# Three of seven aggregation products of a two-layer graph network split once more, and the GpSimd and VectorE work around them reordered

## The chip, the cores and the metric

The kernel runs on one core of a Trainium2 chip. The metric is the device time of one execution, in microseconds. TensorE (PE in the profile) multiplies, VectorE (DVE), ScalarE (ACT) and GpSimd (POOL) do the elementwise work, and the queue of SyncE (SP) issues most of the transfers between DRAM and the on-chip memory, SBUF. Products land in PSUM, which has eight banks of 512 float32 columns.

## The reference

Two layers on `x`, float32 of shape (8, 2048, 256), with a sparse weighted adjacency matrix `adj` of 2048 x 2048. Everything is computed in float32.

```
# layer 0
A_norm = A + I
deg    = A_norm.sum(0) + A_norm.sum(1) - diagonal(A_norm)
A_hat  = A_norm * rsqrt(deg)[:, None] * rsqrt(deg)[None, :]
agg    = einsum('nm,bmd->bnd', A_hat, x)            # aggregation
h      = relu(batchnorm(agg @ W1.T + b1))           # 256 -> 512
out    = batchnorm(h @ W2.T + b2)                   # 512 -> 256
x      = layernorm(x + out)
# layer 1: attention of four heads, scores masked where adj == 0
q, k, v = split(x @ W)
x      = layernorm(x + softmax(q k^T / 8 + mask) v)
```

## The kernel before

The kernel runs in stages: it reads `adj`, turns it and sums its rows and columns (0 to about 58 us); it aggregates and applies the first linear layer (58 to about 997 us); it applies the second linear layer (to about 1225 us); the rest is the attention. The change lies in the second stage.

**The aggregation.** The adjacency matrix, turned, lies in SBUF in quarters `T[k, (i, j)]`, each of 128 partitions x 8 x 512 (half of the summed nodes by 512 of the output nodes). `k` is 0 or 1: two passes, each with its own 2 x 512 output nodes. A batch of `x` is loaded in halves of 1024 nodes by 128 features, a `Form` of 128 x 8 x 128 (4 KB per partition); there are nine places for forms, `x0` to `x8`, handed out from the list `free`. A unit `(k, b, d)` treats two batches, `b` and `b + 1`, for half `d` of the 256 features; there are 2 x 4 x 2 = 16 units, and the two units of a pair (d = 0, 1) fill the same output tiles `ag`. In a unit the four blocks (two batches by two halves of nodes) are multiplied with the four quarters by Winograd's variant of Strassen's algorithm: seven products in place of eight, with sums and differences ("forms") on both sides. The forms of `x` are `S[v, 1]` to `S[v, 4]`, made by `s1` to `s4` on GpSimd; those of the adjacency are `T[k, 2]` to `T[k, 4]`, made once per pass by `t2` to `t4` on VectorE; `T[k, (0, 1)]` has been replaced by its difference to `T[k, (0, 0)]`. A `product` is eight matmuls of 128 x 128 by 512 columns into one PSUM bank (four banks, `psa`, line 363). Their order is p1, p6, p2, p7, p4, p5, p3; as each ends, VectorE adds it into `ag` with the partial sums u1, u2, u3 (ScalarE copies p1).

**Scaling.** The symmetric normalization is applied to the inputs by `scale` (GpSimd, line 333) and to the outputs by multiplying each 128 x 512 block of `ag` with `dbc` (GpSimd, lines 492, 517, 528, 536).

**The linear layer.** After the second unit of a pair, `linear` multiplies the aggregated pair with `W1`, again by seven products (line 412, banks `psh`), one batch at a time: `linear(.., 1)` at the end of the unit, `linear(.., 0)` after the first product of the next unit (the list `later`). GpSimd makes its four forms per batch (`linear_form`, line 402), VectorE adds into the tiles `h0` and `h1`, two transfers of 1 MB store them, and `bn_stats` is taken.

**The order of the work.** The stage stands under a manual schedule: each engine executes in the order in which the program names the operations, and waits at an operation until what it needs is there. So the loads (SP), the scalings and forms (POOL) and the additions (DVE) keep the order of the code. A place of a form or tile can be written again only once its last reader has finished. At the end of every second unit, `mask_of` (line 186) writes a byte mask of a quarter for the attention, through the tile `m8`. In the last unit of the first pass (`turn`) the quarters of the second pass are fetched (`fetch`), their mask, difference and forms are made (lines 186, 510, 371, 375, 379).

## Time and profile before

| what | us |
|---|---|
| median of three runs | 3534.34 (3533.58 to 3535.65) |
| the profiled execution, its own time | 3534.78 |
| its span in the profile | 3532.8 |
| PE busy in the span | 3497.7 |
| DVE, ACT, POOL busy | 2106.0, 1583.5, 2335.7 |
| POOL busy in 300 to 600 us (aggregation) | 148.96 |
| one product of line 363 (16 records) | 6.86 |
| a POOL operation of 128 x 512 / 128 x 1024 / a scaling of 128 x 1024 | 1.27 / 2.35 / 1.90 |
| a DVE addition of 128 x 512 from PSUM | 0.69 |

An fp32 matmul shows as two records with two weight loads (PEld) beside them. Times in the profile are microseconds from the span's start; a line number is that of the kernel before; "idle before" is the time for which an engine waited, with what released it. The duration of a matmul record includes its way through the array, so that records overlap; the pitch from start to start is what counts.

### The profile page before, as it was taken

The page shows a single profiled execution, that of the slowest core. Times are in us where ns is not written, and L with a number is a line of the kernel's source. Part 1 is how long each engine was busy: PE and PEld are TensorE (multiplying, and loading weights), DVE is VectorE, ACT ScalarE, POOL GpSimd, SP SyncE. Part 2 cuts the span into 40 slices and gives each one's busy share as a digit, 9 for nine tenths or more (in the row PEclk, how much of TensorE's full clock was granted, in tenths as well). Part 3 has the DMA queues.
Part 4 walks back from the last instruction along what each step waited for, and adds up shares of the span by engine and source line. Part 5 has one row for each costly group of instructions (what it writes and reads, how often), then busy time and mean ns, then how long its engine had stood idle before and what let it go on. Part 6 is the DMA issues. An engine that isn't in the chain of part 4 may idle for free. (4 is left out here: it accounts for less than half of the span.)

```text
span 3532.8 us, 55461 instructions
## 1 busy us (share of the span) xinstructions
PE 3497.7 (99%) x22483; PEld 1474.0 (42%) x22483; DVE 2106.0 (60%) x3128; ACT 1583.5 (45%) x1952; POOL 2335.7 (66%) x1588
## 2 busy tenths in 40 slices
PE   8999999999999999999999999999999999999998
PEld 5444444444444443434443444443444344444332
DVE  6224343441446656766766776676676677677666
ACT  5000000000034455665665665566566566566555
POOL 4544374535347647787777687778677777777777
PEclk9999999999999999999999999999999999999999
DMA  9122342221257345666576666566566556565555
GB/s 345 54 78 75 98 149 83 72 81 51 89 197 267 146 93 107 132 125 127 115 148 118 119 134 133 116 137 131 114 132 135 117 122 141 115 120 124 116 108 121
DMA packets 197578, 440.17 MB, mean 125 GB/s; under 512 B 14128, under 2 KB 121152, under 8 KB 186944
## 3 DMA queue, kind: packets, MB, share of 16 engines
q0 software_dynamic: 64656, 239.37, 36.0%
q1 hardware_dynamic: 132048, 196.11, 16.2%
q8 instruction: 178, 2.92, 0.3%
q10 hardware_dynamic: 608, 1.06, 0.1%
q14 instruction: 88, 0.72, 0.1%
HBM read 126.62 MB, written 75.51 MB: 57 GB/s over the span
## 5 line engine op out<-in xcount | busy, mean ns | idle before, releaser
L955 DVE SCALAR_TENSOR_TENSOR prob<-mask,st 128x1024 f32<-128x1024 uint8 x1024 | 1241.8, 1217 | 412.1 <-PE st L943 410.0
L961 ACT ACTIVATE prob<-prob 128x1024 f32<-128x1024 f32 x1024 | 1080.5, 1056 | 738.5 <-DVE prob L955 693.2
L973 PE MATMUL out_ps<-prob,v 64*64 64x512 f32 x8192 | 1066.6, 591 | 3.0 <-DVE ot L1001 2.0
L943 PE MATMUL st<-qt,kt 64*64 64x512 f32 x8192 | 1066.0, 591 | 0.1
L996 POOL TENSOR_TENSOR acc<-acc,prob 128x1024 f32<-128x1024 f32 x317 | 827.7, 2611 | 4.9
L363 PE MATMUL pa<-t,x 128*128 128x512 f32 x1792 | 773.2, 593 | 2.8 <-ACT t L239 2.8
L983 POOL DMA_DIRECT2D prob<-prob x447 | 404.4, 930 | 532.2 <-PE out_ps L973 446.0
L943 PEld LDWEIGHTS st<-qt,kt 64*64 64x64 f32 x8192 | 306.5, 133 | 574.9 <-issue 476.7
L973 PEld LDWEIGHTS out_ps<-prob,v 64*64 64x64 f32 x8192 | 305.6, 133 | 544.2 <-issue 489.9
L363 PEld LDWEIGHTS pa<-t,x 128*128 128x128 f32 x1792 | 340.9, 190 | 431.8 <-issue 427.0
L985 POOL TENSOR_TENSOR acc<-acc,prob 128x1024 f32<-128x1024 f32 x126 | 298.3, 2367 | 9.7
L492 POOL TENSOR_TENSOR ag<-ag,dbc 128x512 f32<-128x512 f32 x16 | 20.3, 1266 | 313.0 <-DVE ag L491 285.9
L472 ACT COPY ag<-pa 128x512 f32<-128x512 f32 x16 | 9.4, 588 | 448.4 <-PE pa L363 432.7
L421 ACT COPY h<-ph 128x512 f32<-128x512 f32 x28 | 16.4, 586 | 416.7 <-PE ph L412 416.7
L994 POOL TENSOR_TENSOR acc<-prob 128x1024 f32<-128x1024 f32 x64 | 171.4, 2677 | 1.0 <-DMA prob<-prob 1.0
L1049 DVE SCALAR_TENSOR_TENSOR x<-pm,ri,x 128x64 f32<-128x64 f32 x512 | 109.5, 276 | 86.2 <-PE pm L1041 86.2
L762 ACT ACTIVATE x<-x,ln_nm,ln_rs 128x256 f32<-128x256 f32 x256 | 137.6, 586 | 7.5 <-POOL ln_nm L758 7.5
L877 PE MATMUL pm<-x1t,wq 128*128 128x512 f32 x272 | 132.5, 610 | 2.6 <-ACT x1t L845 2.4
L891 PE MATMUL pm<-wq,x1t 128*128 128x128 f32 x1024 | 125.1, 275 | 0.0
L891 PEld LDWEIGHTS pm<-wq,x1t 128*128 128x128 f32 x1024 | 119.4, 192 | 2.5 <-ACT x1t L845 1.7
L1001 DVE TENSOR_TENSOR ot<-out_ps,ot 128x512 f32<-128x512 f32 x64 | 44.2, 691 | 126.6 <-ACT ot L1000 126.6
L877 PE MATMUL st<-x1t,wq 128*128 128x512 f32 x240 | 119.0, 618 | 0.0
(161 smaller groups left out, 2944.9 us busy)
## 6 DMA issues: line engine op xcount, KB each, us to landing
prob<-prob POOLq DMA_DIRECT2D x447, 512.0 KB, 4.8
x<-in_x_dram SPq DMA_DIRECT2D x92, 512.0 KB, 6.8
h_d<-h SPq DMA_DIRECT2D x28, 1024.0 KB, 4.2
t<-h_d SPq DMA_DIRECT2D x28, 1024.0 KB, 8.2
a<-in_adj_dram SPq DMA_DIRECT2D x16, 1024.0 KB, 5.2
y_d<-ag SPq DMA_DIRECT2D x32, 512.0 KB, 2.6
out_dram<-x SPq DMA_DIRECT2D x31, 512.0 KB, 3.6
yt<-y_d SPq DMA_DIRECT2D x28, 512.0 KB, 3.3
```

The lines of the kernel that those rows point to most:

```text
L363: nc.tensor.matmul(pa, s.t[:, m, :], t[:, m, :], start=(m == 0), stop=(m == HT - 1))
L762: nc.scalar.activation(self.t[:, i, :], self.t[:, i, :], AF.Identity, bias=self.nm[:, i : i + 1], scale=self.rs[:, i : i + 1],)
L877: nc.tensor.matmul(pm, wq[:, d, wcols], xt[:, d, cols], start=(d == 0), stop=(d == ND - 1))
L891: nc.tensor.matmul(pm[:, j * P : (j + 1) * P], xt[:, d, t * P : (t + 1) * P], wq[:, d, wcols], start=(d == 0), stop=(d == ND - 1),)
L943: nc.tensor.matmul(st[r * HD : (r + 1) * HD, h, :], kt[hs, j * P + r * HD : j * P + (r + 1) * HD], qt[hs, cols], start=True, stop=True,)
L955: nc.vector.scalar_tensor_tensor(p, mask[:, j, cols][:, None, :].to_broadcast([P, 2, CH]), MASKED, st, op0=ALU.mult, op1=ALU.add,)
L961: nc.scalar.activation(probs[g], probs[g], AF.Exp)
L973: nc.tensor.matmul(outs[u][hs, r, :], inp.qkv[b, hp][2][rs, j, hs], probs[g][rs, h, :], start=(j == 0), stop=(j == NT - 1),)
L983: nc.gpsimd.dma_start(probs[g - 1], probs[g], accum_op=ALU.add)
L985: nc.gpsimd.tensor_add(accs[u], accs[u], probs[g])
L994: nc.gpsimd.tensor_add(accs[v], probs[g - 7], probs[g - 5])
L996: nc.gpsimd.tensor_add(accs[v], accs[v], probs[g - 5])
```

## The change

Units with d = 0 now compute only p1, p6, p2 and p7. The other three products are left over for the unit with d = 1, which computes each of them for both units at once, as seven "inner" products: the two forms (of d = 0 and d = 1) are stacked to a 2 x 2 matrix of blocks with the two halves of the summed nodes, and the quarter of the adjacency to one with the halves of its columns. An inner product is four matmuls of 256 columns. Class `Inner` makes the inner forms: of the stacked forms on GpSimd into four tiles `narrow0` to `narrow3` of 128 x 512 (`s12`, `s3`, `s4`), of the quarter on VectorE into two tiles `wide0` and `wide1` of 128 x 1024 (`t2`, `t3`, `t4`). The sums are gathered in a form `sums` and then added to one or two output tiles (`targets`). While one set of inner products runs, the forms of the next (`follower`) are made. `narrow` and `wide` are the former `h0` and `h1` in smaller tiles, stored by six transfers.

With it the order changes. In units with d = 0, the forms of the next unit are scaled after p6. In units with d = 1, the scalings of the next forms come after those of the first inner set, s1 and s3 in the middle of the second set (`aside`), beside the scaling of the output by rows (`by_rows`); a last scaling stands after it, and s2 and s4 after `linear`. At the turn, the mask and the difference of the new quarter are cut into six slices, given out among the inner products (`extra`), and t3 and t4 move behind `linear(.., 0)` of the next unit. The masks of the other quarters are made at the end of units with d = 0, into `wide0`; the first of these units in a pass also replaces the right upper block of three quarters by a difference, in place. There is a tenth place for forms, and `m8` is gone.

```diff
-    free = [f"x{i}" for i in range(9)]
+    free = [f"x{i}" for i in range(10)]
...
-            nc.sync.dma_start(h_d[cs[0]], lo)
+            for f in range(2):
+                nc.sync.dma_start(h_d[cs[0]][:, 2 * f : 2 * f + 2, :], los[f])
...
-            nc.sync.dma_start(h_d[cs[1]], hi)
+            for f in range(NH):
+                nc.sync.dma_start(h_d[cs[1]][:, f, :], hi[f])
...
+        M = HT // 2
+        H2 = CH // 2
+        def inner_t(k, tk, j, c):
+            return T[k, tk][:, j * M : (j + 1) * M, c * H2 : (c + 1) * H2]
+        class Inner:
+            def __init__(self, k, vs, key, tk, e, targets):
+                self.k, self.key, self.tk, self.e, self.targets = k, key, tk, e, targets
+                self.forms = [S[(v, *key)] for v in vs]
+            def a(self, i, j):
+                return self.forms[i].t[:, j * M : (j + 1) * M, :]
+            def b(self, j, c):
+                return inner_t(self.k, self.tk, j, c)
+            def place_t(self, e):
+                return wide(e).rearrange("p a b -> p (a b)").rearrange("p (m n) -> p m n", m=M)
+            def t2(self):
+                self.y2 = self.place_t(self.e)
+                nc.vector.tensor_sub(self.y2, self.b(1, 1), self.b(0, 1))
+            def t3(self):
+                self.y3 = self.place_t(1 - self.e)
+                nc.vector.tensor_sub(self.y3, self.y2, self.b(0, 0))
+            def t4(self):
+                nc.vector.tensor_sub(self.y2, self.b(1, 0), self.y2)
+            def place_s(self, n):
+                return narrow(n).rearrange("p (m n) -> p m n", m=M)
+            def s12(self):
+                self.x1, self.x2 = self.place_s(0), self.place_s(1)
+                nc.gpsimd.tensor_add(self.x1, self.a(1, 0), self.a(1, 1))
+                nc.gpsimd.tensor_sub(self.x2, self.x1, self.a(0, 0))
+            def s3(self):
+                self.x3 = self.place_s(2)
+                nc.gpsimd.tensor_sub(self.x3, self.a(0, 0), self.a(1, 0))
+            def s4(self):
+                self.x4 = self.place_s(3)
+                nc.gpsimd.tensor_sub(self.x4, self.a(0, 1), self.x2)
+            def run(self, place, follower=None, extra=(), aside=()):
+                extra = list(extra)
+                c = place.rearrange("p a b -> p (a b)").rearrange("p (d c) -> p d c", d=ND)
+                c11, c12, c21, c22 = (c[:, i, j * H2 : (j + 1) * H2] for i, j in HALVES)
+                def more():
+                    f = extra.pop(0) if extra else None
+                    if f:
+                        f()
+                def product(s, t):
+                    p = psa.tile([P, CH], F32, name="pa")[:, :H2]
+                    for m in range(M):
+                        nc.tensor.matmul(
+                            p, s[:, m, :], t[:, m, :], start=(m == 0), stop=(m == M - 1)
+                        )
+                    return p
+                p1 = product(self.a(0, 0), self.b(0, 0))
+                nc.scalar.copy(c21, p1)
+                p2 = product(self.a(0, 1), self.b(1, 0))
+                nc.vector.tensor_add(c11, p2, c21)
+                more()
+                p6 = product(self.x2, self.y2)
+                self.t4()
+                nc.vector.tensor_add(c12, p6, c21)
+                p5 = product(self.x1, self.b(0, 1))
+                more()
+                if follower:
+                    follower.s12()
+                p7 = product(self.x3, self.y3)
+                nc.vector.tensor_add(c22, p7, c12)
+                nc.vector.tensor_add(c12, p5, c12)
+                if follower:
+                    follower.t2()
+                    follower.s3()
+                for f in aside:
+                    f()
+                p4 = product(self.a(1, 1), self.y2)
+                nc.vector.tensor_add(c21, p4, c22)
+                nc.vector.tensor_add(c22, p5, c22)
+                more()
+                p3 = product(self.x4, self.b(1, 1))
+                nc.vector.tensor_add(c12, p3, c12)
+                for dst, src in self.targets:
+                    nc.vector.tensor_add(dst, c, src)
+                more()
+                if follower:
+                    follower.t3()
+                    follower.s4()
+                for f in self.forms:
+                    f.done()
...
+            def load(i, j):
+                nb, nd = units[w][1:]
+                S[w, i, j] = load_form(nb + i, j, nd)
+            def by_rows(c, j):
+                for half in range(ND):
+                    t = ag[c][:, half, :]
+                    nc.gpsimd.tensor_mul(t, t, dbc[0][:, j, :])
+            def next_forms():
+                for ij in ((0, 0), (1, 0), (1, 1)):
+                    scale(w, *ij)
+                s1(w)
             def do_p6():
                 p6 = product(S[v, 2], T[k, 2])
                 nc.vector.tensor_add(u2, p6, u1)
+                if not (d or first):
+                    next_forms()
+                elif d and not last:
+                    load(1, 0)
+                if turn:
+                    fetch(k + 1, (0, 1), 4)
             p1 = product(S[v, 0, 0], T[k, (0, 0)])
             for f in later:
                 f()
             later = []
             nc.scalar.copy(u1, p1)
-            if not last:
-                nb, nd = units[w][1:]
-                S[w, 0, 0] = load_form(nb, 0, nd)
-                S[w, 1, 0] = load_form(nb + 1, 0, nd)
-                S[w, 1, 1] = load_form(nb + 1, 1, nd)
+            if not d:
+                for ij in ((0, 0), (1, 0), (1, 1), (0, 1)):
+                    load(*ij)
+            elif not last:
+                load(0, 0)
             if turn:
                 fetch(k + 1, (0, 0), 0)
             if first:
...
                 t4(0, 6)
             else:
                 do_p6()
-            if turn:
-                fetch(k + 1, (0, 1), 4)
             p2 = product(S[v, 0, 1], T[k, (1, 0)])
             nc.vector.tensor_add(c11, p2, u1)
+            if first:
+                next_forms()
+                do_p6()
+                s2(w)
             nc.gpsimd.tensor_mul(c11, c11, dbc[0][:, 0, :])
-            if first:
-                p3 = product(S[v, 4], T[k, (1, 1)])
-                do_p6()
-            if not last:
-                S[w, 0, 1] = load_form(nb, 1, nd)
-                for ij in ((0, 0), (1, 0), (1, 1)):
-                    scale(w, *ij)
+            if not d:
+                if not first:
+                    s2(w)
+                scale(w, 0, 1)
+            elif not (last or turn):
+                load(1, 1)
             if turn:
                 fetch(k + 1, (1, 1), 2)
-            if d and not last:
-                for i in range(2):
-                    linear_form(ag, i, 1)
+            if d:
+                inner = [
+                    Inner(k, (v - 1, v), key, tk, n % 2, [(ag[c], ag[u]) for c, u in cs])
+                    for n, (key, tk, cs) in enumerate((
+                        ((1, 1), 4, [((1, 0), (1, 1))]),
+                        ((1,), (0, 1), [((1, 1), (1, 1)), ((0, 1), (0, 1))]),
+                        ((4,), (1, 1), [((0, 1), (0, 1))]),
+                    ))
+                ]
+                inner[0].t2()
+                inner[0].t3()
+                inner[0].s12()
+                inner[0].s3()
+                inner[0].s4()
             p7 = product(S[v, 3], T[k, 3])
             nc.vector.tensor_add(u3, p7, u2)
+            if not d:
+                s3(w)
+                s4(w)
+                n = v % (len(units) // NK) // ND
+                if n < 3:
+                    mask_of(k, ((1, 1), (0, 0), (1, 0))[n], wide(0))
+                if n == 0:
+                    for tk in (4, (0, 1), (1, 1)):
+                        t = inner_t(k, tk, 0, 1)
+                        nc.vector.tensor_sub(t, t, inner_t(k, tk, 0, 0))
+                continue
+            sums = Form()
+            extra = []
             if turn:
-                mask_of(k + 1, (0, 1))
-                t1 = T[k + 1, (0, 1)]
-                nc.vector.tensor_sub(t1, t1, T[k + 1, (0, 0)])
+                f, t1 = Form(), T[k + 1, (0, 1)]
+                m8 = as_mask(f.t)
+                def mask_slice(m, f=f, m8=m8, t1=t1, k=k):
+                    here = slice(m, m + M)
+                    nc.vector.tensor_scalar(
+                        m8[:, here], t1[:, here], 0.0, None, op0=ALU.is_equal
+                    )
+                    if m:
+                        mask_out(k + 1, (0, 1), m8)
+                        f.done()
+                def t1_slice(m, t1=t1, k=k):
+                    here = slice(m, m + 2)
+                    nc.vector.tensor_sub(t1[:, here], t1[:, here], T[k + 1, (0, 0)][:, here])
+                extra = [lambda m=m: mask_slice(m) for m in (0, M)]
+                extra += [lambda m=m: t1_slice(m) for m in range(0, HT, 2)]
+                extra = [f for g in extra for f in (g, None)]
+            if not last:
+                for ij in ((0, 0), (1, 0)) if turn else ((0, 0), (1, 0), (1, 1)):
+                    scale(w, *ij)
+            inner[0].run(sums.t, inner[1], extra[:4])
+            if turn:
+                load(1, 1)
+            if not last:
+                load(0, 1)
+            if turn:
+                fetch(k + 1, (1, 0), 6)
+            aside = [lambda: by_rows((1, 0), 0)]
             if not (last or turn):
+                aside += [lambda: s1(w), lambda: s3(w)]
+            inner[1].run(sums.t, inner[2], extra[4:8], aside)
+            by_rows((1, 1), 1)
+            if not last:
+                linear_form(ag, 1, 1)
+                linear_form(ag, 1, 2)
+                if turn:
+                    scale(w, 1, 1)
+                scale(w, 0, 1)
+            inner[2].run(sums.t, None, extra[8:])
+            sums.done()
+            if last:
+                by_rows((0, 1), 1)
+                break
+            linear(k, b, ag, 1)
+            by_rows((0, 1), 1)
+            linear_form(ag, 0, 1)
+            linear_form(ag, 0, 2)
+            later = [lambda k=k, b=b, ag=ag: linear(k, b, ag, 0)]
+            if not turn:
+                s2(w)
+                s4(w)
+            else:
+                t2(k + 1, 5)
                 s1(w)
                 s2(w)
-                s3(w)
-            p4 = product(S[v, 1, 1], T[k, 4])
-            nc.vector.tensor_add(c21, p4, u3)
-            nc.gpsimd.tensor_mul(c21, c21, dbc[0][:, 0, :])
-            if turn:
-                fetch(k + 1, (1, 0), 6)
-                t2(k + 1, 5)
-            if not last:
-                scale(w, 0, 1)
-                if not turn:
-                    s4(w)
-            p5 = product(S[v, 1], T[k, (0, 1)])
-            nc.vector.tensor_add(c22, p5, u3)
-            nc.vector.tensor_add(u2, p5, u2)
-            nc.gpsimd.tensor_mul(c22, c22, dbc[0][:, 1, :])
-            if d and not last:
-                linear_form(ag, 1, 2)
-            if turn:
-                t3(k + 1, 1)
-            if not first:
-                p3 = product(S[v, 4], T[k, (1, 1)])
-            nc.vector.tensor_add(c12, p3, u2)
-            nc.gpsimd.tensor_mul(c12, c12, dbc[0][:, 1, :])
-            n = v % (len(units) // NK)
-            if n in (2, 4, 6):
-                mask_of(k, ((0, 0), (1, 0), (1, 1))[n // 2 - 1])
-            if last:
-                break
-            if d:
-                linear(k, b, ag, 1)
-                linear_form(ag, 0, 2)
-                if turn:
-                    t4(k + 1, 3)
-                    s1(w)
-                    s2(w)
-                later = [lambda k=k, b=b, ag=ag: linear(k, b, ag, 0)]
-                if turn:
-                    later += [lambda w=w: s3(w), lambda w=w: s4(w)]
+                later += [lambda f=f, w=w: f(w) for f in (s3, s4)]
+                later += [lambda k=k: t3(k + 1, 1), lambda k=k: t4(k + 1, 3)]
...
```

## The prediction

> **What bounds the kernel now.** I read the busy shares on the page first, then TensorE in stretches, then the wait list of line 363, then the timeline of the aggregation, engine by engine.
>
> ```profile
> PE 3497.7 (99%) x22483; PEld 1474.0 (42%) x22483; DVE 2106.0 (60%) x3128; ACT 1583.5 (45%) x1952; POOL 2335.7 (66%) x1588
> ...
> 300.00:600.00 300.00, 299.75 (x700) 132.46 (x699) 121.72 (x153) 7.42 (x13) 148.96 (x76) 1.00 0.34 111
> 600.00:900.00 300.00, 300.00 (x701) 132.82 (x700) 102.81 (x153) 9.67 (x17) 141.71 (x84) 1.00 0.22 69
> ```
>
> TensorE (PE) is the bound: busy for 299.75 and 300.00 us of these two stretches of the aggregation. GpSimd (POOL) is busy for half of them. Time can be won only by taking work from PE, and is lost as soon as PE waits.
>
> ```profile
> 396.04 3.60 PE L412 MATMUL ph<-ag,w1s 128*128 128x512 f32 x8
> ...
> 408.06 7.03 PE L363 MATMUL pa<-t,x 128*128 128x512 f32 x16
> 414.92 3.60 PE L412 MATMUL ph<-ag,w1s 128*128 128x512 f32 x8
> ...
> 1242.15 1.95 PE L891 MATMUL pm<-wq,x1t 128*128 128x128 f32 x16
> ```
>
> From the timeline of PE: one aggregation product (8 matmuls, 16 records) occupies 414.92 - 408.06 = 6.86 us, 429 ns a record; a 128-column record has a pitch of (1950 - 275)/15 = 112 ns, where 275 is the duration of one. A pair of units (d = 0, 1) is 14 products and two `linear` of 12.0 us, 120.1 us; the row scalings of line 492 recur every 120.17 us (321.55 to 441.71), so nothing is lost in it.
>
> ```profile
> 498.73 5.37 DVE L510 TENSOR_TENSOR t<-t,t 128x4096 f32<-128x4096 f32 x1
> 504.03 0.68 DVE L516 TENSOR_TENSOR ag<-pa,ag 128x512 f32<-128x512 f32 x1
> 504.63 4.88 DVE L371 TENSOR_TENSOR t<-t,t 128x4096 f32<-128x4096 f32 x1
> 509.54 0.69 DVE L526 TENSOR_TENSOR ag<-pa,ag 128x512 f32<-128x512 f32 x1
> ...
> 505.19 5.46 POOL L517 TENSOR_TENSOR ag<-ag,dbc 128x512 f32<-128x512 f32 x1
> 510.61 1.89 POOL L333 TENSOR_TENSOR x<-x,dinv 128x1024 f32<-128x1024 f32 x1
> 512.46 5.45 POOL L528 TENSOR_TENSOR ag<-ag,dbc 128x512 f32<-128x512 f32 x1
> 517.99 1.26 POOL L402 TENSOR_TENSOR g<-ag 128x512 f32<-128x512 f32 x1
> ```
>
> These rows, of the turn to the second half, carry the forecast. VectorE (DVE) subtracts tile from tile in SBUF, and POOL's 128x512 operation takes 5.46 us instead of 1.26: it ends 1.14 us after DVE does (510.65 against 509.51). DVE waits likewise: 4.88 instead of 4.42 alone. So an SBUF-only tensor operation of DVE and one of POOL exclude each other, and they take turns. DVE additions that read PSUM (0.69) slow nobody. One DVE operation of 1024 elements (1.22 us, line 350) that cuts into busy POOL costs it 1.07 (a quarter of 4.29, what line 371 still took after POOL's end at 505.22) + 1.14 - 1.23 (POOL's pitch at 512) = 1.0 us. In a plain pair of before DVE has no such operation but the mask.
>
> **The change, part by part.**
>
> *PE.* Per pair six products go, 6 x 6.86 = 41.2 us. Three inner ones come, each 7 x 4 matmuls of 256 columns, 168 records. The only row of 256 columns (line 1014) uses 32 columns of the array and overlaps its neighbours; bounds are half the 512 record, 214 ns, and twice the 128 record, 224. I take 217, nearer the half, since the excess over proportion shrinks with width. That is 36.5 us (36.0 to 37.6): 4.7 saved per pair (3.5 to 5.1), 38 in eight pairs if nothing waits.
> The Trainium skill, TensorE: Matmul & The Clock Gate, "Back-to-back issue gap", has N/2.4 + 2.5 ns a warm pass; an estimate with two passes a record is 218 ns, and 4.5 saved.
>
> *DVE.* Per inner set three forms and one or two target additions, each 1024 elements in SBUF, all excluding POOL, and seven PSUM additions of some 0.35. DVE itself has room.
>
> *POOL.* Twelve 128x512 forms more per pair, 15 us; half idle before, POOL has room on average. The order is what counts. Take t = 0 at p1 of a unit with d = 1. POOL's queue waits at the scaling of c11 until p2 ends (20.6), though its next forms need nothing of it. From 21.4: nine operations of 1.25, three scalings of 1.87 and five exchanges of 1.0 end at 43.3. PE is then in the second inner set; its p5 ends at 27.4 + 11 x 1.74 = 46.5, and only then may POOL overwrite x1. So the first part is hidden with 3 us to spare. The second part is not. From 46.7 until the third form of `linear` (G3) POOL has, in order: x1, x2, x3, two scalings of (1,0), s1, s3, x4, two scalings of (1,1), two linear forms, one scaling by 1.88, G3. That is 11 x 1.25 + 2 x 2.33 + 1.9 = 20.3, with six exchanges (t2, two targets, t3, t4, the last target) 26.3: ready at 73.0. PE from 46.5 has ten inner products (17.4) and six `linear` matmuls (5.1) before it needs G3: 69.0. PE loses 4.0 us per plain pair: some of it at p7 and p4 of the third inner set (DVE's t3 and t4 stand behind POOL's s1 and s3, 2.3 us each), the rest at G3. With 0.2 for restarts a plain pair nets -4.7 + 4.2 = -0.5; six of them, -3.0 us. Bounds: without any exchange POOL needs 20.5, below PE's 22.5, and the whole 4.7 stays; with each exchange at full durations (1.22 + 1.37 - 1.23 = 1.36) the loss is 6.2. I take the turn's rows, the only ones with both engines contending.
>
> *The rest of the queues.* The loads of the next unit stand behind `linear`'s stores on SP as before (six stores instead of two, 0.3 us each); they land some 7 us later, and POOL finishes s2 8 us before p6 needs it. Masks move to the end of units with d = 0, where POOL's s3 and s4 have 20 us: nothing. The finer stores of h: nothing, p1 (6.9 us) and a landing of 4.2 lie between.
>
> *The turn pair.* Six sliced operations of DVE join the exchanges, s1 and s3 leave: G3 about 0.9 later than in a plain pair; in the next unit t3 and t4 (4.4 each) hold POOL, and s2 comes about 0.6 late for p6. Before, this pair took 120.68. Net +0.5 (bounds -4.7 and +5).
>
> *The last pair* has no next forms, so POOL keeps up: -4.4.
>
> *The start.* Before, unit 0 had seven products; now it has four. POOL scales two forms at once, after W1 at 64.8, and so cuts between DVE's s1, s2 and s4: t2 ends at 76.0 instead of 72.75, and p6, formerly behind p3, is wanted at 73.3. A wait of 2.7 us. Then s2 waits for the third load, which is behind the mask's write (64.1 + 20.8 us to landing) in the same tile: about 0.6. The only pause of this length in the trace is the 2.76 us before the first product, which then took 8.57 us instead of 7.03, 1.5 lost at a granted clock of 0.50 (58 to 60 us). I add half of it, 0.8. Start +4.1 (bounds 0 and +14, see below).
> The Trainium skill, same page, "What's actually happening", has the clock fall after an idle window of about 3.4 us; by it the wait of 2.7 costs no clock, and the start is 3.3.
>
> *The end.* The last addition is followed by 1.22 + 2.5 us of scaling; the next matmuls ask for it after three pairs, 5.2 us: hidden. The load of W2 waits for that scaling, some 2 us later than before; about 0.7 of it shows (bounds 0 and 2).
>
> Sum: -3.0 + 0.5 - 4.4 + 4.1 + 0.7 = -2.1 us. The profiled execution took 3534.8 (span 3532.8, 2.0 around it), 0.4 above the median of 3534.34. Forecast: **3532 us**.
>
> **Rivals.**
> *B, POOL is not in the way.* For it: POOL is idle half the time, and the exclusion is seen only with operations of 4096 elements and, once, 1024 (line 346 took 1.54 instead of 1.22). Against: that one case obeys it too. Eight times -4.7, start +3.3, end +0.7: 3501; half the loss: 3515.
> *C, the exchanges are dearer.* At 1.36 each, 2.2 us more in each of seven pairs: 3532 + 15 = 3547, slower. It decides from 1.3 us per pair on. For it: many small operations, each handed over; against: the turn's rows.
> *D, the start.* A load issued there took up to 12.8 us to land. Landing at 97.7, scaling, s1, s2 and two exchanges end near 107, ten after p6 wants them: 3542. Against: by then the writes queued ahead are through.
>
> **How the numbers follow.** 0.2% is 7 us, about what a measurement of this kernel can tell from no change. Forecast 0.38, own range 3525 to 3541 (0.05 of it below, 0.02 above the 7 us); B 0.32, faster; C 0.20 (0.02 within); D 0.10 (0.02 within). Faster 0.37, same 0.35, slower 0.28. The range takes in most of B and C: 3505 to 3548.
>
> **What the changed profile would show.** 256-column records at 214 to 224 ns; in a plain pair, PE idle before p7 and p4 of the third inner set, released by DVE forms, and before G3's matmuls, released by POOL; POOL nearly without gaps from the second inner set's p5 to G3; rows of 2.3 us where DVE's forms alone need 1.2; a wait of 2 to 3 us before unit 0's p6; a row period near 119.6. The forecast is wrong if POOL has gaps in that stretch, or if PE waits elsewhere: for PSUM, for a load, or at s2 of every unit.

## The result, and the profile after

The changed kernel takes 3531.28 us (median; 3530.56 to 3532.99), the kernel before, run in turn with it, 3535.56 (3533.58 to 3537.18). The ratio is 0.9989, with a 95% interval of 0.998 to 0.9998: some 4 us less, below the 0.2% that was called measurable, against a forecast of 3532.

From the page of the changed kernel, and from the same two stretches as before (a row of a stretch gives its length, then the busy time of PE, PEld, DVE, ACT and POOL, and last the granted TensorE clock, the DMA share and GB/s):

```profile
PE 3469.0 (98%) x23059; PEld 1582.8 (45%) x23059; DVE 2357.6 (67%) x3346; ACT 1592.4 (45%) x1976; POOL 2530.2 (72%) x1684
...
300.00:600.00 300.00, 292.55 (x848) 161.27 (x847) 192.22 (x216) 9.86 (x20) 200.24 (x103) 0.99 0.34 111
600.00:900.00 300.00, 290.68 (x918) 173.22 (x917) 186.68 (x231) 12.82 (x26) 213.46 (x119) 1.00 0.22 69
```

PE had been busy for all but 0.25 of these 600 us; now it stands idle for 16.8 of them. PE's busy time fell by 28.7 us, the span by 4.0 (3532.8 to 3528.8): what was taken from PE is mostly spent in waiting. The list of PE's waits names for whom (longest at the end of each row; the rows left out were there before, in other stages):

```profile
PE pa L533 <- DVE wide L502: 9.8, 7, 2.4
PE ph L429 <- POOL ag L417: 6.6, 6, 1.1
...
PE pa L533 <- DVE wide L499: 5.8, 7, 1.1
...
PE pa L378 <- DVE t L386: 2.2, 1, 2.2
```

L533 is the inner product, L502 and L499 are its forms t4 and t3 on VectorE, L417 is a linear form of GpSimd, L429 the matmuls of `linear`, L378 the outer product. In a plain pair they lie as follows, on PE from the third inner set to the third form (G3) of `linear`:

```profile
266.67 1.89 PE L533 MATMUL pa<-t,narrow 128*128 128x256 f32 x8
269.34 1.97 PE L533 MATMUL pa<-wide,narrow 128*128 128x256 f32 x8 [0.78 <-DVE wide L499]
272.54 1.99 PE L533 MATMUL pa<-wide,x 128*128 128x256 f32 x8 [1.24 <-DVE wide L502]
274.37 1.89 PE L533 MATMUL pa<-t,narrow 128*128 128x256 f32 x8
...
279.56 1.98 PE L429 MATMUL ph<-g,w1f 128*128 128x512 f32 x4
282.64 1.98 PE L429 MATMUL ph<-ag,w1f 128*128 128x512 f32 x4 [1.09 <-POOL ag L417]
```

The rows are p5, p7, p4 and p3 of the third set, then the second and third group of `linear`. The pitch of inner products that follow each other without a wait is 1.727 us (252.86, 254.59, 256.31 in the second set), 216 ns a record. From start to start, p7, p4, p3 and G3 come 0.94, 1.47, 0.10 and 1.36 late, 3.9 together, of which 3.1 are the waits named and the rest is restarting (the product that follows a waiting one is itself 0.1 late). The period of a plain pair (237.32 to 356.56) is 119.24, against 120.17 before.

POOL and DVE in the same stretch, from the place of x1 coming free to G3:

```profile
256.56 1.26 POOL L509 TENSOR_TENSOR narrow<-x 128x512 f32<-128x512 f32 x1 [3.54 <-PE pa L533]
...
264.79 3.33 POOL L361 TENSOR_TENSOR x<-x,x 128x1024 f32<-128x1024 f32 x1
265.83 3.37 DVE L499 TENSOR_TENSOR wide<-wide,t 128x1024 f32<-128x1024 f32 x1
268.19 3.21 POOL L369 TENSOR_TENSOR x<-x,x 128x1024 f32<-128x1024 f32 x1
269.45 3.03 DVE L502 TENSOR_TENSOR wide<-t,wide 128x1024 f32<-128x1024 f32 x1
271.36 2.25 POOL L518 TENSOR_TENSOR narrow<-x,narrow 128x512 f32<-128x512 f32 x1
...
279.47 1.89 POOL L348 TENSOR_TENSOR x<-x,dinv 128x1024 f32<-128x1024 f32 x1
281.32 1.26 POOL L417 TENSOR_TENSOR ag<-g,ag 128x512 f32<-128x512 f32 x1
```

POOL first waits 3.54 us for p5 and then has no gap until G3 ends at 282.58, 26.0 us later. s1 and s3 (L361, L369) and t3 and t4 (L499, L502) are caught in each other: POOL's take 3.33 and 3.21 instead of 2.35, DVE's 3.37 and 3.03 instead of 1.22.

Two more waits lie outside the plain pairs, at the start (p6 of unit 0) and at the turn (p7, p4 and p3 of its third set):

```profile
76.51 41.75 PE L378 MATMUL pa<-t,x 128*128 128x512 f32 x96 [2.18 <-DVE t L386]
...
508.17 1.97 PE L533 MATMUL pa<-wide,narrow 128*128 128x256 f32 x8 [1.14 <-DVE wide L499]
512.49 3.36 PE L533 MATMUL pa<-wide,x 128*128 128x256 f32 x8 [2.36 <-DVE wide L502]
515.65 2.25 PE L533 MATMUL pa<-t,narrow 128*128 128x256 f32 x8
```

At the turn two products took 3.36 and 2.25 us instead of 1.99 and 1.89. Cut into stretches, the changed kernel's turn shows why:

```profile
510.00:512.50 2.50, 0.14 (x2) 0.01 (x1) 2.50 (x3) 0.00 (x0) 2.50 (x2) 1.00 0.00 0
512.50:514.00 1.50, 1.50 (x5) 1.21 (x6) 1.12 (x3) 0.00 (x0) 1.42 (x2) 0.65 0.00 0
514.00:516.00 2.00, 2.00 (x6) 1.63 (x5) 0.11 (x1) 0.00 (x0) 2.00 (x2) 0.50 0.00 0
516.00:518.00 2.00, 2.00 (x9) 1.67 (x8) 1.94 (x4) 0.00 (x0) 2.00 (x2) 0.91 0.00 0
```

After the pause the clock was granted at half speed for some 3 us. The turn's pair takes 122.03 us (475.79 to 597.82), 1.35 more than before.

The span's 4.0 us then add up from first and last starts in each part: six plain pairs -0.93 each, -5.6; the turn's pair +1.35; the last inner set, 36.63 instead of 41.16, -4.5; from the first product to the first inner set +2.9 (2.18 of it the wait); the second linear layer +0.3; and +1.1 at the step from there into the attention. The attention itself takes 2278.6 us in both. The rest is +0.6 ahead of the first product, which begins at 58.55 instead of 57.92 (at 57.78 to 58.43 in the runs below), and -0.2 behind the last. The +1.1 is clock: behind a pause of 1.61 us, which is there in both kernels, it was granted in full before (second row) and at half speed after (first row).

```profile
1224.00:1226.00 2.00, 2.00 (x6) 0.86 (x5) 1.66 (x6) 1.30 (x2) 0.00 (x0) 0.50 1.06 379
1229.00:1231.00 2.00, 1.98 (x8) 0.77 (x6) 1.97 (x7) 0.45 (x1) 0.14 (x1) 1.00 1.05 374
```

### The profile page after: what moved, and what is told of

The parts are those of the page before. It is cut to its first block, busy times and chain, and to the rows that moved or that the text cites. A ratio compares the mean times of both kernels' runs of the same rounds, so it can differ in the third digit from the quotient of the medians.

```text
span 3528.8 us, 57170 instructions
## 1 busy us (share of the span) xinstructions
PE 3469.0 (98%) x23059; PEld 1582.8 (45%) x23059; DVE 2357.6 (67%) x3346; ACT 1592.4 (45%) x1976; POOL 2530.2 (72%) x1684
## 5 line engine op out<-in xcount | busy, mean ns | idle before, releaser
L378 PE MATMUL pa<-t,x 128*128 128x512 f32 x1024 | 444.6, 594 | 5.8 <-ACT t L245 2.8
L378 PEld LDWEIGHTS pa<-t,x 128*128 128x128 f32 x1024 | 194.7, 191 | 252.5 <-issue 240.7
L348 POOL TENSOR_TENSOR x<-x,dinv 128x1024 f32<-128x1024 f32 x60 | 128.1, 2155 | 121.3 <-DMA x<-in_x_dram 121.3
L539 ACT COPY x<-pa 128x256 f32<-128x256 f32 x24 | 8.9, 373 | 384.8 <-DVE ag L565 209.0
```

Of the source, the lines that this page charges most:

```text
L378: nc.tensor.matmul(pa, s.t[:, m, :], t[:, m, :], start=(m == 0), stop=(m == HT - 1))
```

## The experiments

The theory is that of the prediction: PE is held up by the length of POOL's queue between the second inner set's p5 and G3, with what DVE's operations add to it. Its rivals are: POOL is too slow over the whole pair, whatever the order; the length of single POOL operations is what holds up DVE's forms; DVE's operations cost POOL nothing. All edits are to the changed kernel.

**1. s1 and s3 earlier.** These two forms of the next unit, made by POOL, go from the middle of the second inner set to behind the first.

```diff
-                aside += [lambda: s1(w), lambda: s3(w)]
+                s1(w)
+                s3(w)
```

> GpSimd's s1 and s3 of the next unit stand right after the first inner set's work instead of inside the second's, so that they fall into the 3.5 us for which GpSimd waits for the second set's p5. Theory 'length of the queue': 4.7 us leave the stretch after p5, but s1 and s3 with VectorE's operations between them need some 2.5 to 3 us more than the gap has, so the stretch ends 1.6 us earlier: period of a plain pair 117.5 to 118, six pairs, total about 3522 (3519 to 3524). Rival 'the order of the scalings and next forms does not matter, GpSimd has simply too much work in units with d = 1': the same work in the same unit, period and total unchanged, 3531.

Measured: 3520.72 us (3519.71 to 3521.39), ratio 0.996 (0.9946 to 0.9974); period 117.64. PE in a plain pair:

```profile
384.56 1.97 PE L533 MATMUL pa<-wide,narrow 128*128 128x256 f32 x8 [0.26 <-DVE wide L499]
386.68 1.99 PE L533 MATMUL pa<-wide,x 128*128 128x256 f32 x8 [0.15 <-DVE wide L502]
396.78 1.98 PE L429 MATMUL ph<-ag,w1f 128*128 128x512 f32 x4 [1.10 <-POOL ag L417]
```

The two waits for t3 and t4 are nearly gone; the one for G3 stays. Nothing was taken from POOL's work, only its place was changed, and 10.6 us are won: the order is a cause.

**2. s1 and s3 in halves.** They stay where they are, each as two operations of 128x512.

```diff
-            engine.tensor_add(S[v, 1].t, S[v, 1, 0].t, S[v, 1, 1].t)
+            for c in cuts(halves):
+                engine.tensor_add(S[v, 1].t[:, c, :], S[v, 1, 0].t[:, c, :], S[v, 1, 1].t[:, c, :])
...
-                aside += [lambda: s1(w), lambda: s3(w)]
+                aside += [lambda: s1(w, halves=True), lambda: s3(w, halves=True)]
```

> In the second inner set of a plain pair, GpSimd's s1 and s3 of the next unit (128x1024, 2.35 us each) are each cut into two operations of 128x512; nothing else changes. Theory 'length of the queue': what counts is how long GpSimd needs from the second set's p5 to G3 (26 us against 22.5 on TensorE); cutting makes it 0.2 to 0.3 longer. VectorE's t3 and t4 then get their turn behind operations of 1.25 instead of 2.35, so the waits before p7 and p4 of the third set (0.77 and 1.24 us) all but vanish, but the time comes back before p3 (x4 is late) and before the matmuls on G3: the period of a plain pair stays at 119.2 to 119.6, the total within 3 us of the changed kernel's 3531.3. Rival 'waiting behind long operations': the waits before p7 and p4 are the loss itself; they go and nothing comes in their place: period 117.2, total 12 us lower, 3519.

Measured: 3531.29 us (3530.06 to 3532.26), ratio 0.9989 (0.9979 to 0.9998), as without the edit; period 119.52. PE in a plain pair (line numbers are 5 higher):

```profile
394.10 1.99 PE L538 MATMUL pa<-t,narrow 128*128 128x256 f32 x8 [1.58 <-POOL narrow L523]
399.98 1.98 PE L434 MATMUL ph<-g,w1f 128*128 128x512 f32 x4 [0.46 <-POOL g L422]
403.06 1.98 PE L434 MATMUL ph<-ag,w1f 128*128 128x512 f32 x4 [1.10 <-POOL ag L422]
```

With shorter operations t3 and t4 come in time, and PE waits instead for POOL's own later forms: x4 before p3 (1.58), the second form of `linear` (0.46), G3 (1.10). The sum, 3.14 us, is that of before (3.11). The rival of the long operations falls: the waits only change their names.

**3. The last scaling behind `linear`.**

```diff
-                scale(w, 0, 1)
             inner[2].run(sums.t, None, extra[8:])
...
             linear(k, b, ag, 1)
+            scale(w, 0, 1)
             by_rows((0, 1), 1)
```

> One scaling of 1.89 us, the last one of the next unit, moves on POOL from before the third form of `linear` to behind the last matmuls of `linear`. Theory (the queue's length up to that form is what PE waits for): the wait of 1.09 us there goes, those before p7 (0.78) and p4 (1.24) stay, since they lie earlier in the queue; period 118.0 to 118.2 in place of 119.24, and 3531.3 - 7 x 1.1 = 3524 us. If instead POOL is too slow over the whole pair, the wait only moves to s2 or p6 of the next unit and the time stays within 2 us of 3531.

Measured: 3521.99 us (3520.9 to 3522.92), ratio 0.9965 (0.9953 to 0.9978); period 117.87. The wait for G3 is gone, those before p7 and p4 are still 0.80 and 1.24, and no new one stands in the next unit of a plain pair: POOL is not too slow over the whole pair. The gain per pair is 1.37, the start-to-start loss at G3 (1.36); the expectation had counted only the wait of 1.09.

**4. The first part of the queue.** POOL's four forms of the first inner set are made ahead of p1, in place of behind the scaling of c11, for which POOL's queue waits.

```diff
+                inner[0].s12()
+                inner[0].s3()
+                inner[0].s4()
             p1 = product(S[v, 0, 0], T[k, (0, 0)])
...
                 inner[0].t2()
                 inner[0].t3()
-                inner[0].s12()
-                inner[0].s3()
-                inner[0].s4()
```

> GpSimd's four forms of the first inner set are made before p1 of the unit with d = 1 instead of behind the scaling of c11 after p2; the rest keeps its order. So some 5 us of work leave the busy stretch of GpSimd for a time in which it is idle. Theory 'only the stretch after the second set's p5 counts, since p5 frees the place of x1': GpSimd then only waits some 5 to 8 us longer for that p5; period 119.2 (119.0 to 119.4), total 3531 (within 3 us). Rival 'GpSimd is overloaded from p2 to G3 as a whole': G3 comes up to 5 us earlier, the 4 us per pair vanish, period 115.2 to 116, total 3507 to 3512.

Measured: 3530.94 us (3530.25 to 3532.7), ratio 0.9989 (0.998 to 0.9999); period 119.23, all waits of PE in the plain pair as in the changed kernel. POOL gets through the first part some 2 us earlier and stands idle for as much longer, at the place where it waits for p5:

```profile
375.92 1.26 POOL L509 TENSOR_TENSOR narrow<-x 128x512 f32<-128x512 f32 x1 [5.57 <-PE pa L533]
```

5.57 instead of 3.54, and nothing is won: work taken from ahead of p5 only makes the wait for p5 longer.

**5. The order without the inner products.** The three left-over products are computed plainly, twice each, in the new order; the inner forms are left out.

```diff
-                p1 = product(self.a(0, 0), self.b(0, 0))
...
+                for dd, f in enumerate(self.forms):
+                    p = psa.tile([P, CH], F32, name="pa")
+                    for m in range(HT):
+                        nc.tensor.matmul(
+                            p, f.t[:, m, :], T[self.k, self.tk][:, m, :],
+                            start=(m == 0), stop=(m == HT - 1),
+                        )
+                    for dst, src in self.targets:
+                        nc.vector.tensor_add(dst[:, dd, :], p, src[:, dd, :])
```

> The new order without the inner products: the three products left over for the unit with d = 1 are computed as two plain products each (8 matmuls of 512 columns, VectorE adds each from PSUM into its target), without inner forms on GpSimd or VectorE and without the replaced blocks; loads, scalings, next forms, masks and slices stay where the change put them. The output is the reference's. Theory 'the inner forms in GpSimd's queue eat the gain': the new order by itself is nearly free; a plain pair takes 120.1 to 120.3 us as before without waits, the start costs its 2 to 3 us, total 3536 to 3541. Rival 'the new order itself costs the time' (loads, scalings or masks now in the way): waits remain without the inner forms, plain pairs at 123 to 124, total 3555 to 3565.

Measured: 3540.28 us (3538.73 to 3542.33), ratio 1.0015 (1.0005 to 1.0024). The period is 120.17, that of before, with no wait in a plain pair; the start (2.18 for t2, 0.35 for s2) and the turn (0.84 for s2) remain:

```profile
76.33 20.87 PE L378 MATMUL pa<-t,x 128*128 128x512 f32 x48 [2.18 <-DVE t L386]
97.55 20.87 PE L378 MATMUL pa<-t,x 128*128 128x512 f32 x48 [0.35 <-POOL x L365]
```

So the rearrangement by itself costs about 5 us, by the rows 3.3 at the start and 0.6 at the turn, and in a plain pair it is the inner forms that make POOL late.

**6. The price of an exchange.** The three VectorE forms of the third inner set are left out, so this kernel doesn't compute the reference's result.

```diff
             def t2(self):
+                if self.tk == (1, 1):
+                    self.y2, self.y3 = self.b(1, 0), self.b(0, 0)
+                    return
...
             def t3(self):
+                if self.tk == (1, 1):
+                    return
```

(`t4` likewise.)

> Leaves work out: VectorE's three forms of the third inner set (t2, t3, t4) are not made; its products p6, p7, p4 take blocks of the quarter instead. PE, the targets and all of POOL's own operations stay. It measures the disputed price of an exchange: three of the six exchanges between the second inner set's p5 and the third form of `linear` are gone. Theory (an exchange holds POOL for about 1.0 us): that stretch of POOL falls from the measured 26.0 us to about 23.0, against PE's own 22.5; the waits before p7 and p4 have no cause left, the wait before the third form's matmuls is at most 0.7, the period of a plain pair falls from 119.24 to 116.0 to 116.5, and the time by 6 x 3 + 2 to 3, to 3510 us. Rival (POOL's own operations fill the stretch, the exchanges cost it nothing): p7 and p4 no longer wait, but the third form is ready as late as before, the wait there grows to 3.5 us, period 119, 3530 us.

Measured: 3509.06 us (3507.77 to 3509.28), ratio 0.9928 (0.9911 to 0.9944); period 116.32. POOL at the ends of the stretch, and PE at G3:

```profile
371.27 1.27 POOL L516 TENSOR_TENSOR narrow<-x 128x512 f32<-128x512 f32 x1 [3.54 <-PE pa L540]
...
393.12 1.26 POOL L417 TENSOR_TENSOR ag<-g,ag 128x512 f32<-128x512 f32 x1
...
394.43 1.98 PE L429 MATMUL ph<-ag,w1f 128*128 128x512 f32 x4 [0.82 <-POOL ag L417]
```

POOL has the same operations and now needs 394.38 - 371.27 = 23.1 us in place of 26.0: three exchanges fewer, 0.97 us each. The wait at G3 is 0.82 where at most 0.7 was expected. The rival that DVE costs POOL nothing falls. The Trainium skill, SBUF — State Buffer, "SBUF: two separate sides", calls the port pair that the two engines share an exclusive lock, which one instruction holds to its end while the other engine is blocked; the runs agree (POOL's form of 1.26 us takes 5.31 in run 7, while a VectorE operation of 4.43 us runs), and add the price in a queue without gaps: 0.97 us for a VectorE operation that takes 1.22 alone.

**7. The turn.** The last two slices of the new quarter's difference go from the third inner set to behind `linear`.

```diff
-            inner[2].run(sums.t, None, extra[8:])
+            inner[2].run(sums.t, None)
...
             else:
+                for f in extra[8:]:
+                    if f:
+                        f()
                 t2(k + 1, 5)
```

> At the turn, the last two slices of the difference of the new quarter move from the third inner set to behind `linear`, where they stand ahead of the forms of that quarter. Theory (at the turn those slices stand ahead of t4 on VectorE): the wait before p4 falls from 2.36 to about 1.1, that before p7 (1.14) stays; with the shorter pause the following matmuls are back at 1.99 us (3.36 and 2.25 in the changed kernel, 1.6 lost). Then s2 comes later for the next unit's p6, by up to 2.5 us. The turn pair takes 119.2 to 121.7 in place of 122.03, and the whole 3529 to 3531 us: too little for the time, so the rows decide. If the slow matmuls come from elsewhere than the pause, they are slow again.

Measured: 3530.76 us (3529.97 to 3532.11), ratio 0.9989 (0.998 to 0.9999), no difference by the time. By the rows the pair takes 121.42 instead of 122.03. The wait of 2.36 before p4 (1.1 was expected to be left) and the slow products are gone (1.99 and 1.89 us), 3.9 us from start to start; 3.3 came back, in a wait of 2.01 at a place that was not foreseen and one of 0.74 at G3, with the restarts. DVE, POOL and PE there:

```profile
535.09 4.43 DVE L386 TENSOR_TENSOR t<-t,t 128x4096 f32<-128x4096 f32 x1
535.34 5.31 POOL L417 TENSOR_TENSOR ag<-g,ag 128x512 f32<-128x512 f32 x1 [4.84 <-PE ph L429]
...
540.70 1.98 PE L429 MATMUL ph<-ag,w1f 128*128 128x512 f32 x4 [2.01 <-POOL ag L417]
```

t2 of the new pass, now later, begins 0.25 us before the third form of the second batch, and that form of 1.26 us takes 5.31. s2, which was expected to be late, was not: its wait stays at 0.85.

**8. All moves together.** The edits of 1, 3, 4 and 7, and the first two scalings for unit 1 on ScalarE:

```diff
-                    scale(w, *ij)
+                    scale(w, *ij, on_act=first and ij != (1, 1))
```

> All moves together: s1 and s3 of the next unit behind the first inner set, the last scaling behind `linear`, two slices of the turn behind `linear`, the forms of the first inner set ahead of p1, and the first two scalings for unit 1 on ScalarE. Theory (only the order of POOL's and VectorE's queues takes the gain away): no wait of PE over 0.3 us in a plain pair, its period 120.17 - 4.9 + 0.2 = 115.5 us; the start wins 2 us, the turn 0 to 2; 3531.3 - 6 x 3.7 - 3 = 3506 us. Rival (POOL and VectorE have not the room for these forms in a pair, 81 us of POOL's 119 busy): PE waits elsewhere, and the period stays at 117.6, the value with s1 and s3 moved alone; 3519 us.

Measured: 3518.75 us (3517.09 to 3522.33), ratio 0.9958 (0.9944 to 0.9972); period 117.53: by the numbers, the rival's. G3 no longer waits, but PE waits in the second set at p4, where it had not before, and in the third at p7 and p4 (0.26 and 0.15 in run 1):

```profile
375.71 1.99 PE L533 MATMUL pa<-wide,x 128*128 128x256 f32 x8 [0.51 <-DVE wide L502]
387.21 1.97 PE L533 MATMUL pa<-wide,narrow 128*128 128x256 f32 x8 [0.87 <-DVE wide L499]
389.33 1.99 PE L533 MATMUL pa<-wide,x 128*128 128x256 f32 x8 [0.15 <-DVE wide L502]
```

With POOL running ahead, s1 and s3 meet t3 and t4 of the second set squarely (3.37 and 3.04 us; 2.29 and 2.62 in run 1). The start lost too: p6 of unit 0 waits for 0.79 instead of 2.18, but s2 of unit 1 is 2.71 late, where the changed kernel had no such wait, and behind that pause the clock was granted at 0.50, another 1.7 us. Whether it is lack of room or this meeting, the next run tells.

**9. Only 1 and 3 together.**

```diff
-                aside += [lambda: s1(w), lambda: s3(w)]
+                s1(w)
+                s3(w)
...
-                scale(w, 0, 1)
             inner[2].run(sums.t, None, extra[8:])
...
             linear(k, b, ag, 1)
+            scale(w, 0, 1)
```

> The two moves that each won alone, together and nothing else: s1 and s3 of the next unit behind the first inner set, the last scaling behind `linear`. Theory (what counts is which operations stand on POOL between the second inner set's p5 and the third form): the wait for that form (1.10 us with s1 and s3 moved alone) goes, the waits before p7 (0.26) and p4 (0.15) stay, since the scaling stands behind both; period 117.64 - 1.36 = 116.3 us, 3520.7 - 7 x 1.36 = 3511 us. If the period stays at 117.5, as with all moves together, POOL or VectorE has no room left in the pair, whatever the order; 3520 us.

Measured: 3511.92 us (3510.59 to 3512.58), ratio 0.9934 (0.9918 to 0.9951): the fastest of the kernels that compute the whole, and faster than both. The period is 116.26. PE in a plain pair, where only these two waits are left:

```profile
382.77 1.97 PE L533 MATMUL pa<-wide,narrow 128*128 128x256 f32 x8 [0.24 <-DVE wide L499]
384.88 1.99 PE L533 MATMUL pa<-wide,x 128*128 128x256 f32 x8 [0.15 <-DVE wide L502]
```

The period (116.3 expected) and the time (3511) came out as the queue's length foretold. The rival of run 8 falls: there is room in the pair for all the work. In plain pairs run 8 differs from this one by edit 4 alone (the other two act at the start and at the turn), so edit 4, which was worth nothing by itself, there cost 1.3 us a pair. That it did so by the meeting with t3 and t4 is read from the rows; no run takes it apart.

**10. t3 ahead of the target additions**, on top of 9 and with the edit of 7.

```diff
+                if follower:
+                    follower.t3()
+                    follower.s4()
                 for dst, src in self.targets:
                     nc.vector.tensor_add(dst, c, src)
                 more()
-                if follower:
-                    follower.t3()
-                    follower.s4()
```

> As with the two moves, and besides: VectorE makes t3 of the next inner set ahead of the target additions in place of behind them, and the last two slices of the turn move behind `linear`. Theory (p7 waits only because t3 stands behind two additions that nobody needs soon): the wait before p7 is gone, that before p4 is 0 to 0.3, since t4 now follows the additions at once; period 115.4 to 116.1, about 0.4 less than with the two moves alone, and 0.6 at the turn: 3507 us. If t4 is held up by what t3 has let ahead, the wait moves from p7 to p4 and the time is that of the two moves.

Measured: 3513.39 us (3512.62 to 3514.87), ratio 0.9939 (0.9923 to 0.9956); period 116.26, not 115.4 to 116.1. ScalarE and PE in a plain pair:

```profile
384.11 0.37 ACT L539 COPY x<-pa 128x256 f32<-128x256 f32 x1 [14.18 <-DVE ag L568]
384.63 1.97 PE L533 MATMUL pa<-wide,narrow 128*128 128x256 f32 x8 [0.70 <-ACT x L539]
```

t3 is in time, and p7 waits all the same, for a copy: ScalarE copies the third set's p1 into `sums`, which the target additions of the second set (L568), now later, are still reading; and p7 is to use the PSUM bank that the copy empties. The additions "that nobody needs soon" were needed. At the turn the same wait is 2.17 us. In this run, as in run 6, the start's wait for t2 was 3.88 instead of 2.18: t2 was no later, but the first product took 7.1 us instead of 8.8, the clock being granted in full, so PE came to p6 1.7 us earlier.

## Why the prediction was right

The time was right, and for the reason given, the wait of PE for POOL's queue in a plain pair; that the whole came so close is in part luck, since errors in other terms cancel. The sum (-2.1 foretold, the span measured -4.0) goes term by term as follows.

- *PE.* 216 ns a record were measured, 217 taken. The inner sets of a pair take 36.27 us for 41.16, 4.9 saved (predicted 4.7).
- *The plain pair.* Predicted: POOL needs 26.3 us from x1 to G3; measured 26.0. Predicted: three waits, before p7, p4 and G3, losing 4.2 with restarts; measured those three, 4.0 (4.9 - 0.93). Net -0.93 instead of -0.5, six times: 2.6 us of the difference, all of it in two terms that were 0.2 off each. Predicted: the first part hidden with 3 us to spare; measured 3.54, and run 4 showed that more of it is worth nothing.
- *The price of an exchange.* 1.0 was taken from one pair of rows at the turn; run 6 measured 0.97.
- *The start.* Predicted +4.1: a wait of 2.7 before p6, 0.6 for s2, 0.8 of clock. Measured +2.9: the wait was 2.2, with its restart 2.5; s2 cost 0.3 (it was 0.22 to 0.74 late in runs 1 to 5); the first product was 0.2 longer; and the clock stayed at 1.00 after the pause. That last is chance: in run 9 the clock fell after the same pause, and took 1.7 us. Neither run shows the half loss that was predicted.
- *The turn.* Predicted +0.5, measured +1.35: this is the queue term whose mechanism was incomplete. The prediction placed the loss at G3 and at s2 (0.6, measured 0.85); most of it fell on p7 and p4, where the slices stand ahead of t3 and t4 on DVE, and then on the clock, about 1.6 us, which the prediction had not set down there.
- *The last pair and the end.* -4.5 for -4.4, +0.3 for +0.7. The +1.1 at the step into the attention, again of clock, had no term. The two losses of clock that were not foreseen, 2.7 us, make up for the plain pairs' extra 2.6.

Rival B (POOL not in the way, 3501 or 3515) falls with the waits; it is run 9 that shows what it would have taken, two lines in another place. Rival C (dearer exchanges, 3547) falls with the price of 0.97, rival D (a late load at the start, 3542) with the first scaling of that load, which it had wait for a landing at 97.7:

```profile
88.66 1.90 POOL L348 TENSOR_TENSOR x<-x,dinv 128x1024 f32<-128x1024 f32 x1 [17.63 <-DMA x<-in_x_dram]
```

## What to carry to other kernels

When work is taken from the bounding engine and given to an engine that is half idle, add up the second engine's queue between two events that fix it, the place that comes free and the result that is waited for, and compare that with what the bounding engine has to do in between; its busy share (here 200 of the 300 us from 300 to 600) doesn't tell. Count in it every operation that stands there only by the order of the code, for these can be moved for nothing: two such moves here made 4 us into 23. Look before each move at what will run beside it: in run 8 a further move, worth nothing by itself, put forms beside others and gave 1.3 us a pair back.

## What was not expected of the hardware

The clock was granted at half speed after a pause of only 2.36 us at the turn (0.65 and 0.50 in the rows above), some 3 us long, costing 1.6 us. Not always: in run 9 the same two pauses, 1.13 and 2.35 us, left it at 1.00, as these rows of its turn show:

```profile
502.00:504.20 2.20, 0.00 (x0) 0.00 (x0) 2.20 (x2) 0.00 (x0) 2.20 (x2) 1.00 0.00 0
504.20:506.00 1.80, 1.77 (x8) 1.59 (x9) 1.15 (x3) 0.00 (x0) 1.72 (x2) 1.00 0.00 0
```

Of the six kernels with this pause, in one profiled execution each, four lost clock (the changed kernel and runs 1, 3 and 4) and two did not (2 and 9); run 7, without it, kept 1.99 and 1.89 us. At the start it was as mixed: after the pause of 2.18 us the changed kernel kept its clock (first row), and run 9, after 2.19, did not (second row).

```profile
76.50:78.50 2.00, 1.99 (x5) 1.04 (x6) 2.00 (x2) 0.00 (x0) 0.00 (x0) 1.00 1.05 442
76.50:78.50 2.00, 2.00 (x3) 0.66 (x2) 2.00 (x2) 0.00 (x0) 0.00 (x0) 0.50 0.93 393
```

So it was before the first product too, where the prediction took its 1.5 us from: with a pause of 2.76 to 2.77 us in every kernel, the clock fell in nine kernels of twelve and stayed in runs 6, 8 and 10. The Trainium skill, TensorE: Matmul & The Clock Gate, "What's actually happening", has the clock fall after at least one idle window of about 3.4 us, and has the window run freely, whatever the kernel does. If all of the window had to be idle, none of these pauses would cost anything; the rows differ from that. That the window's phase decides would fit the mixed outcome, but no run here shows the window, and it stays open.
